# GpSimd adds lam ahead of the first logarithms of the large blocks, one logarithm for a quarter of the heads

## The chip, the core and the metric

The kernel runs on one core of one Trainium2 chip. The metric is the device time of one execution in microseconds. A core has five engines, each with its own queue of instructions, worked off in order: TensorE (PE in the profile), VectorE (DVE), ScalarE (ACT), GpSimd (POOL) and SyncE (SP, which issues the DMAs here).

## The reference, cut to what matters

Two layers follow each other on x of 8 images x 512 rows x 128 columns. The second, a six-layer local attention with feed-forward parts, is not touched. The first is an attention of 16 heads whose weights are not a softmax: each row's lam is found by four Newton steps, and the weight is 1/(lam - s).

```python
s = jnp.einsum('bhnd,bhmd->bhnm', Q, K) * scale
lam = s_masked.max(-1) + 1.0
for _ in range(num_iter):          # 4
    d = jnp.maximum(lam[..., None] - s, EPS)
    w = jnp.where(mask, d ** (-q), 0.0)          # q = 1
    f = w.sum(-1) - 1.0
    fp = -q * jnp.where(mask, d ** (-q - 1.0), 0.0).sum(-1)
    lam = lam - f / fp
d = jnp.maximum(lam[..., None] - s, EPS)
p = jnp.where(mask, d ** (-q), 0.0)
p = p / p.sum(-1, keepdims=True)
return jnp.einsum('bhnm,bhmd->bhnd', p, V)
```

## The kernel before

The first part, which ends about 1,620 us after the start, works on blocks. A block is 128 rows of one image, all 16 heads; block rb sees W = (rb + 1) x 128 keys, so blocks 3 and 2 are the large ones (W = 512 and 384) and blocks 1 and 0 the small ones. The heads of a block are worked on in four tiles, j = 0 to 3, of four heads each ("a quarter of the heads"). A partition holds a row and a head; in the free dimension lie four pieces a = 0 to 3, one per 32 rows, of 416, 448, 480 and 512 elements in block 3 (1,856 in all) and of 288, 320, 352 and 384 in block 2 (1,344), because later keys are left out. `ns` holds the negated scores, `lam` one number for each partition and piece.

A Newton step on one tile is Ln(ns + lam), then exp(-x), which gives 1/d, then sums by `bn_stats` (line 301); when the four tiles are done, a chain of small VectorE operations (lines 305 to 316) gives the new `lam`. How `lam` is added differs by size:

- Small blocks (`few`, line 290): GpSimd adds it, with `add_lam` (line 264), into tiles `df`, of which there are four; one Ln on ScalarE (line 294) then covers the whole tile.
- Large blocks: ScalarE adds it as the bias of the logarithm. The bias is one number per partition, so each of the four pieces needs a Ln of its own (line 298). The result goes to a tile `d` of the pool `dp`, which has two buffers (line 115). One Exp (line 299) then covers the whole tile.

After the last step the weights proper are made in the same way: `attend_add` (line 318) lets GpSimd add `lam` into a tile `da`, of which there are three; `attend_weigh` does Ln and Exp on ScalarE (lines 325, 326); `attend_sum` transposes on TensorE (line 339), masks on VectorE (line 342), multiplies with the values (line 351).

The loop goes over stages w (line 392). A stage is two blocks of one image: blocks 3 and 0, then blocks 2 and 1, then the next image. In stage w three things run side by side, in each of the steps k = 0 to 3: the Newton step k of the stage's two blocks, tile k of the weights and sums of the blocks of the stage before (`before`), and tile k of the scores of the blocks of the next stage (`nxt`, lines 238 to 257, written to `ns` by VectorE at line 254). The first `lam` of a stage (`first_lam`, lines 270 and 272) needs the smallest `ns` of all four tiles. `add_lams` (line 276) puts the small block's adds for one k ahead. At the change to the stage of blocks 2 and 1 the next image is projected (`project`, line 191): normalisation (`rstd` at line 97, `xn` at 102, copies `xnT` at 107), products with the weights (`qj` at 199, `kn` at 205), after which its scores can begin. When a block is done, `attend_end` copies `oT` on ScalarE (line 378) for the output product.

The order of the instructions on each engine is set by the scheduler that builds the program; it interleaves the parts of a step. Each engine then keeps to that order, and waits where an operand or a buffer is not ready. A tile's buffer is ready when all readers of its former content are done: for `d`, the `bn_stats` of two tiles earlier.

Of the kernel before, what the change touches and what calls it, by code (L numbers as in the profile page):

```python
# [49 lines left out]
def tile_kernel(  # L50
# [59 lines left out]
    with ExitStack() as c1:  # L110
# [111 lines left out]
        def keys(W, a):  # L222
            return W - Q * (3 - a)

        def pieces(d, W):

            at = [sum(keys(W, c) for c in range(a)) for a in range(5)]
            return [d[:, at[a] : at[a + 1]] for a in range(4)]
# [30 lines left out]
        def add_lam(t, d, j):  # L259

            W = t["W"]
            for a, (o, n) in enumerate(zip(pieces(d, W), pieces(t["ns"][j], W))):
                by = t["lam"][:, 4 * j + a : 4 * j + a + 1]
                nc.gpsimd.tensor_tensor(o, n, by.to_broadcast([P, keys(W, a)]), ALU.add)  # L264
# [19 lines left out]
        def newton(t, k):  # L284
            W, lam = t["W"], t["lam"]

            st = sm.tile([P, H, 2, 3], F32, name="stw")
            for j in range(4):
                ns = t["ns"][j]
                few = W <= 2 * P  # L290
                d = t["df"][j] if few else dp.tile([P, 4 * W - 6 * Q], F32, name="d")
                dv, nv = pieces(d, W), pieces(ns, W)
                if few:
                    nc.scalar.activation(d, d, AF.Ln)
                else:
                    for a in range(4):
                        c = 4 * j + a
                        nc.scalar.activation(dv[a], nv[a], AF.Ln, bias=lam[:, c : c + 1])  # L298
                nc.scalar.activation(d, d, AF.Exp, scale=-1.0)  # L299
                for a in range(4):  # L300
                    nc.vector.bn_stats(st[:, 4 * j + a].rearrange("p u k -> p (u k)"), dv[a])  # L301

            mean = st[:, :, :, 1]
            s1 = sm.tile([P, H, 2], F32, name="s1")
            nc.vector.tensor_tensor(s1, mean, st[:, :, :, 0], ALU.mult)
            q2 = st[:, :, :, 0]
            nc.vector.tensor_tensor(q2, s1, mean, ALU.mult)
            sw2 = sm.tile([P, H], F32, name="sw2")
            nc.vector.tensor_reduce(sw2, st[:, :, :, 0:3:2], axis=AX.XY, op=ALU.add)
            sw = sm.tile([P, H], F32, name="sw")  # L310
            nc.vector.scalar_tensor_tensor(
                sw, s1[:, :, 0], -1.0, s1[:, :, 1], ALU.add, ALU.add
            )
            nc.vector.reciprocal(sw2, sw2)
            nc.vector.tensor_tensor(sw, sw, sw2, ALU.mult)
            nc.vector.scalar_tensor_tensor(lam, sw, 0.0, lam, ALU.max, ALU.add)  # L316
# [75 lines left out]
        for w in range(len(work) + 1):  # L392
            before, now, nxt = now, nxt, []
            if w + 1 < len(work):
                b, rbs = work[w + 1]
                nxt = [block(b, rb, proj) for rb in rbs]
            for t in now:
                first_lam(t)
            for k in range(NUM_ITER):
                if now:  # L400
                    add_lams(now[1])
                for u in range(2):
                    if before:
                        attend_add(before[u], k)
                    if nxt:
                        scores(nxt[u], k)
                    if now:
                        newton(now[u], k)
                    if ready:
                        attend_sum(*ready)  # L410
                        ready = None
                    if before:
                        attend_weigh(before[u])
                        ready = (before[u], before[u]["d"], k)
            if w + 2 < len(work) and work[w + 2][1][0] == 3:
                if ready:
                    attend_sum(*ready)
                    ready = None
                proj = project(work[w + 2][0])
# [375 lines left out]
    t = -1  # L795
# [94 lines left out]
```

## Time and profile before

Three runs took 5203.93, 5205.71 and 5205.83 us, a median of 5205.71. The profiled execution took 5202.6 us, of which 5200.9 us are its span from the first to the last instruction.

| engine | busy us | share of the span | instructions |
|---|---|---|---|
| PE | 4371.9 | 84% | 44173 |
| DVE | 4428.0 | 85% | 11788 |
| ACT | 3822.1 | 73% | 6698 |
| POOL | 3204.4 | 62% | 3919 |

How to read the lines that follow. Times are microseconds from the start of the span unless marked ns. The rows of slices cut the span into 40 equal pieces, and each digit is the busy share of an engine in one of them, in tenths, 9 standing for 90% and more. A row of a table by window has the window, its length, then busy time with the number of instructions in brackets for PE, the weight loads of PE, DVE, ACT and POOL, then the granted TensorE clock, the DMA share and GB/s. A row of a group has the line, the engine, the operation, output and input with their sizes, the count, the busy time in us, the mean in ns and the idle time of the engine just before. A row of a timeline has the start, the length of what was merged, the engine, the line, the operation and the count; in square brackets stands the time that the engine was idle before it, and who ended it.

### The profile page before, as it was taken

Reading aid. Unit: us, or ns where it says so; the run is one execution under the profiler, and the core shown is the slowest. Engines: PE = TensorE matmul, PEld = TensorE weight load, DVE = VectorE, ACT = ScalarE, POOL = GpSimd, SP = SyncE. Lnnn points to the kernel's source line nnn. Section 1 sums busy time; section 2 is a strip of 40 time slices with the busy share of each in tenths; the row PEclk is TensorE's granted clock in tenths of the full one; section 3 lists DMA queues with packets and bytes.
Section 4 is the critical chain, followed back from the end, with each engine's and each line's share of the span. In section 5 each row is a group of like instructions: output and inputs, shape, how many; then the busy total and the mean of one; then the engine's idle time right before and its main releaser. Section 6 shows DMA issues by size and latency. Waiting matters only on the chain.

```text
span 5200.9 us, 116009 instructions
## 1 busy us (share of the span) xinstructions
PE 4371.9 (84%) x44173; PEld 2617.0 (50%) x44173; DVE 4428.0 (85%) x11788; ACT 3822.1 (73%) x6698; POOL 3204.4 (62%) x3919
## 2 busy tenths in 40 slices
PE   4556656556555999999999999999999999999998
PEld 1223322233323566666666666666666666666665
DVE  7788889888887888888888888888888888888886
ACT  6899989899997566666666666666666666666665
POOL 2444434435445777777777777677777777776774
PEclk7666667667666999999999999999999999999999
DMA  0000000000001211221212112121112212122121
GB/s 9 1 5 1 5 5 1 5 5 1 3 3 33 50 46 42 53 55 40 48 40 62 42 45 50 45 58 38 47 45 58 50 38 51 44 56 54 44 55 37
DMA packets 115041, 177.85 MB, mean 34 GB/s; under 512 B 13072, under 2 KB 38456, under 8 KB 114488
## 3 DMA queue, kind: packets, MB, share of 16 engines
q1 hardware_dynamic: 114488, 170.45, 13.4%
q8 instruction: 351, 5.75, 0.5%
q14 instruction: 202, 1.65, 0.1%
HBM read 21.52 MB, written 4.19 MB: 5 GB/s over the span
## 4 chain that ended last, share of the span: by engine, by line
DVE 37%; PE 33%; ACT 20%; POOL 6%; issue 3%; DMA 0%; ACTq 0%; POOLq 0%; SPq 0%; DVEq 0%
DVE qr L556 6%; DVE ss L546 6%; PE m L540 5%; DVE qn L548 5%; DVE stw L301 5%; ACT d L298 4%; DVE rs L640 3%; PE po L662 3%; PE pv L576 3%; ACT d L299 3%; PE pT L652 3%; PE acc L675 3%; PE s L623 2%; PE y L746 2%; PE s L249 2%
## 5 line engine op out<-in xcount | busy, mean ns | idle before, releaser
L560 POOL TENSOR_TENSOR qn<-qn,qr 128x512 f32<-128x512 f32 x768 | 975.3, 1270 | 447.6 <-DVE qr L556 316.0
L642 POOL TENSOR_TENSOR pr<-pr,rs 128x768 f32<-128x768 f32 x384 | 564.1, 1469 | 502.7 <-DVE rs L641 249.9
L568 POOL TENSOR_TENSOR qn<-qn,ss 128x512 f32<-128x512 f32 x768 | 784.6, 1042 | 56.6 <-ACT ss L565 56.4
L540 PE MATMUL m<-wqkv,xs 128*128 128x512 f32 x1536 | 751.5, 607 | 76.7 <-ACT qT L604 66.5
L264 POOL TENSOR_TENSOR df<-ns,lam 128x32 f32<-128x32 f32 (+7 forms) x1024 | 396.9, 425 | 607.9 <-DVE lam L316 388.0
L546 DVE TENSOR_REDUCE ss<-sq 128x8 f32<-128x512 f32 x768 | 521.2, 679 | 255.9 <-ACT sq L545 254.2
L298 ACT ACTIVATE d<-ns,lam 128x416 f32<-128x416 f32 (+7 forms) x1024 | 559.5, 615 | 65.9 <-DVE stw L301 28.4
L556 DVE TENSOR_TENSOR qr<-m,tab 128x256 f32<-128x256 f32 x1536 | 570.9, 412 | 0.0
L669 ACT COPY oT<-po 128x512 f32<-128x512 f32 x384 | 223.9, 583 | 460.9 <-PE po L662 460.9
L301 DVE BATCH_NORM_STATS2 stw<-d 128x6 f32<-128x416 f32 (+7 forms) x1024 | 514.6, 561 | 55.4 <-ACT d L299 54.9
L249 PE MATMUL s<-kn,qj 32*32 32x160 f32 (+15 forms) x4096 | 423.7, 492 | 152.0 <-DVE mn L254 137.5
L339 PE MATMUL dTp<-ident,da 128*128 128x128 f32 x1280 | 295.4, 372 | 294.0 <-issue 71.8
L548 DVE TENSOR_TENSOR qn<-m,tab 128x512 f32<-128x512 f32 x768 | 514.0, 669 | 0.0
L264 POOL TENSOR_TENSOR da<-ns,lam 128x416 f32<-128x416 f32 (+15 forms) x512 | 310.6, 638 | 329.1 <-PE dTp L339 253.9
L640 DVE TENSOR_REDUCE rs<-pr 128x8 f32<-128x768 f32 x384 | 363.6, 947 | 171.5 <-ACT pr L634 171.5
L545 ACT ACTIVATE sq<-m 128x512 f32<-128x512 f32 x768 | 433.7, 602 | 66.0 <-PE m L540 52.6
L604 ACT COPY qT<-ptq 128x512 f32<-128x512 f32 x768 | 414.0, 583 | 83.5 <-PE ptq L599 78.7
L599 PEld LDWEIGHTS ptq<-ident,qn 128*128 128x128 f32 x3072 | 359.1, 141 | 218.9 <-issue 113.6
L662 PE MATMUL po<-prT,v 96*64 96x64 f32 x12288 | 443.2, 225 | 0.1
L653 ACT COPY prT<-pT 96x512 f32<-96x512 f32 x768 | 428.0, 587 | 13.2 <-PE pT L652 7.8
L576 PE MATMUL pv<-wqkv,xs 128*128 128x512 f32 x768 | 432.8, 645 | 0.5 <-DVE qr L556 0.5
L634 ACT ACTIVATE pr<-pr 128x768 f32<-128x768 f32 x384 | 326.7, 851 | 136.4 <-DVE pr L630 135.5
(139 smaller groups left out, 9252.2 us busy)
## 6 DMA issues: line engine op xcount, KB each, us to landing
v<-v SPq DMA_DIRECT2D x192, 512.0 KB
v<-v SPq DMA_DIRECT2D x96, 256.0 KB
v<-v SPq DMA_DIRECT2D x96, 192.0 KB
wqkv<-in_L_ffn_Wqkv_dram SPq DMA_DIRECT2D x36, 256.0 KB
wo<-in_L_ffn_Wo_dram SPq DMA_DIRECT2D x12, 256.0 KB
xb<-in_L_attn_x_dram SPq DMA_DIRECT2D x8, 256.0 KB
x<-xb SPq DMA_DIRECT2D x8, 256.0 KB
xr<-x SPq DMA_DIRECT2D x8, 256.0 KB
```

Source lines behind the costliest of these rows:

```text
L264: nc.gpsimd.tensor_tensor(o, n, by.to_broadcast([P, keys(W, a)]), ALU.add)
L298: nc.scalar.activation(dv[a], nv[a], AF.Ln, bias=lam[:, c : c + 1])
L301: nc.vector.bn_stats(st[:, 4 * j + a].rearrange("p u k -> p (u k)"), dv[a])
L540: nc.tensor.matmul(m.rearrange("p h e -> p (h e)"), lhsT=lhsT, rhs=wqkv[:, t, :], start=True, stop=True,)
L546: nc.vector.tensor_reduce(ss[:, t, :], sq, axis=AX.X, op=ALU.add)
L548: nc.vector.tensor_tensor(qc, m, tab[:, 2 * t, c, :].unsqueeze(1).to_broadcast([P, HH, DHL]), ALU.mult)
L556: nc.vector.tensor_tensor(qr[:, :, u, :], mh[:, :, 1 - u, :], sw.unsqueeze(1).to_broadcast([P, HH, hd]), ALU.mult,)
L560: nc.gpsimd.tensor_tensor(qc, qc, qr.rearrange("p h u e -> p h (u e)"), ALU.add)
L568: nc.gpsimd.tensor_tensor(qc, qc, ss[:, t, :].unsqueeze(2).to_broadcast([P, HH, DHL]), ALU.mult)
L576: nc.tensor.matmul(pv, lhsT=lhsT, rhs=wqkv[:, 2, :], start=True, stop=True,)
L642: nc.gpsimd.tensor_tensor(flat, flat, rs.unsqueeze(2).to_broadcast([P, 2 * NT, KB]), ALU.mult)
L662: nc.tensor.matmul(po[e * DHL : (e + 1) * DHL, n * QB : (n + 1) * QB], lhsT=g["v3"][:, n, h * DHL : (h + 1) * DHL], rhs=prT[:, e, n // 2, ...
```

## The change

At the first Newton step (k = 0) of a large block GpSimd adds `lam` to the tile's four pieces, into the same `d`, by the helper that the small blocks use; ScalarE then does one Ln in place over the whole tile. The steps k = 1 to 3 and the small blocks are as before. No buffer count changes.

```diff
                 few = W <= 2 * P
                 d = t["df"][j] if few else dp.tile([P, 4 * W - 6 * Q], F32, name="d")
                 dv, nv = pieces(d, W), pieces(ns, W)
-                if few:
+                if k == 0 and not few:
+                    add_lam(t, d, j)
+                if few or k == 0:
                     nc.scalar.activation(d, d, AF.Ln)
                 else:
                     for a in range(4):
```

## The prediction

> **What bounds the kernel.** The page came first, for the part that the change touches. In the row of slices one slice is 130 us; the first 12 to 13 of 40 (0 to about 1,620 us) are the first part, with ScalarE (ACT) at 9 tenths, VectorE (DVE) at 8, GpSimd (POOL) at 4.
>
> ```profile
> DVE  7788889888887888888888888888888888888886
> ACT  6899989899997566666666666666666666666665
> POOL 2444434435445777777777777677777777776774
> ```
>
> A table of busy time by window then gave one period, two stages or one image. ACT is busy 184.9 of 201 us, POOL 89.4: GpSimd looks half free.
>
> ```profile
> 700.00:901.00 201.00, 119.28 (x1052) 60.44 (x1044) 172.34 (x632) 184.86 (x268) 89.37 (x194) 0.69 0.01 4
> ```
>
> Next the groups by form, for prices (last numbers: busy us, mean ns, idle before):
>
> ```profile
> L299 ACT ACTIVATE d<-d 128x1856 f32<-128x1856 f32 x128 | 222.3, 1736 | 0.0
> L298 ACT ACTIVATE d<-ns,lam 128x512 f32<-128x512 f32 x128 | 90.5, 707 | 0.0
> L264 POOL TENSOR_TENSOR da<-ns,lam 128x512 f32<-128x512 f32 x32 | 33.2, 1036 | 0.0
> ```
>
> The timelines were last, since an average cannot say where the 8% of ACT's idle time sits. It sits at the stage changes, and the longest piece there already waits for GpSimd:
>
> ```profile
> 733.27 1.53 ACT L298 ACTIVATE d<-ns,lam 128x320 f32<-128x320 f32 x3
> 738.95 1.75 ACT L325 ACTIVATE da<-da 128x1856 f32<-128x1856 f32 x1 [4.14 <-POOL da L264]
> ...
> 774.55 0.90 ACT L294 ACTIVATE df<-df 128x832 f32<-128x832 f32 x1 [2.71 <-POOL df L264]
> ```
>
> The same 4.14 stands at 537.98, 939.96 and 1141.16, one period apart. So ACT bounds the first part by its work, but at k = 0 of the stage of blocks 2 and 1 it is held by GpSimd, and that is the k which gets more GpSimd work.
>
> **What the change removes.** Four logarithms of a piece each become one over the whole tile, for 16 large blocks x 4 tiles: 192 ACT instructions less. From recorded means, block 3 has 631+654+680+707 = 2,672 ns against 1,736 (one activation of 1,856), block 2 has 524+548+575+602 = 2,249 against 1,311: 0.94 us each, 60 us for 64. But records overlap. Starts are what counts:
>
> ```profile
> 698.98 2.40 ACT L298 ACTIVATE d<-ns,lam 128x416 f32<-128x416 f32 x4
> 701.29 0.45 ACT L299 ACTIVATE df<-df 128x320 f32<-128x320 f32 x1
> 701.65 1.73 ACT L299 ACTIVATE d<-d 128x1856 f32<-128x1856 f32 x1
> 703.28 0.81 ACT L294 ACTIVATE df<-df 128x320 f32<-128x320 f32 x2
> ```
>
> Four take 701.29-698.98 = 2.31 us, one takes 703.28-701.65 = 1.63: 0.68. For block 2, 1.86 (797.98 to 799.84) against 1.22: 0.64. So 32 x 0.68 + 32 x 0.64 = **42 us** at most.
>
> **What it adds.** Four adds per tile on GpSimd: 876+929+982+1,036 = 3.82 us for block 3, 664+717+770+824 = 2.98 for block 2 by the means, 3.70 and 2.86 by a run of four on the timeline (780.36; 843.49). 32 x 3.70 + 32 x 2.86 = **210 us** on POOL, 13 us per stage, all in one quarter of it. No DMA or TensorE work is added or moved. The order of the changed program's instructions shows the adds and the 192 missing logarithms, so the change does what it says.
>
> The new wait: ACT's logarithm waits for POOL's adds, and POOL's adds for a `d` buffer. There are two, so tiles 0 and 1 can be filled once the statistics (L301) of tiles 2 and 3 of the last k have read theirs; tiles 2 and 3 must wait for the statistics of tiles 0 and 1. POOL is in order. Its new queue at k = 0 of blocks 2 and 1 is: d0, df0, d1, df1 to df3, da (block 3), da (block 0), three pieces of the next da, the memsets, d2, one piece of da, d3.
>
> **The stage of blocks 2 and 1, on the clock of before.** POOL now:
>
> ```profile
> 725.25 2.00 POOL L264 TENSOR_TENSOR df<-ns,lam 128x160 f32<-128x160 f32 x4 [9.53 <-DVE stw L301]
> 729.31 5.94 POOL L264 TENSOR_TENSOR df<-ns,lam 128x160 f32<-128x160 f32 x12 [2.06 <-DVE sw L309]
> 735.21 5.64 POOL L264 TENSOR_TENSOR da<-ns,lam 128x416 f32<-128x416 f32 x9
> ```
>
> - POOL: the buffer for d0 is free at 724.0 (statistics at 721.72, 2.27 us). d0 to 726.9, df0 728.9, d1 731.7, df1 to df3 737.7, da of block 3 741.3 (before 738.9), da of block 0 742.4, next da 745.2, memsets 746.6, d2 749.5, da 750.4, d3 753.3. No gap: 29 us of adds against some 15 of ACT's own work.
> - ACT: d0 and d1 are ready when it comes (729 to 733.5), but da is not until 741.3, d2 749.5, d3 753.3. In before the last log of tile 3 ended at 751.0; here it is 754.4. The 2.6 us saved are gone, and more.
> - Behind the log of d2 stand the two normalisations (`rstd`, L97). They ran at 742.6; now they come at 750.6. From there before's chain takes 748.7-742.6 = 6 us to the copy of `xnT`, 756.4 to `kn` and 760.8 to the first new `ns`. With +8 the `ns` come at about 768.5. In DVE's queue the block-1 update of `lam` stands behind them. Before has it at 772.2; now fewer statistics remain behind `ns` (about 3 us made up): 777.7. The 2.71 stall above is the wait for that update: the adds then end at 780.0 instead of 774.5, and ACT goes on to its next logs at 782.8 instead of 777.3, with 0.36 of work done ahead. **+5.1 us** for each of the 6 such stages with a projection. From there ACT has no idle time until 835 in before, so nothing gives it back.
> - In the two without it (first and last image) only the later da: 741.3-738.9 = **+2.4** each.
>
> **The stage of blocks 3 and 0.** d0 runs 826.5 to 830.2 and d1 to 833.9, hidden under the small block's activations. df0, da and df1 then end 2.1 us later than before; DVE's `ns` waits for that da (837.08 now, 1.11 idle) and goes to 839.1, the update of `lam` behind it to 842.0. POOL's next da needs that: 844.1; the one after it 847.0; d2 850.7; d3 854.4. ACT wants d2 at 847.2, waits 3.5 us, and also gets the copy `oT` 2 us later (841 for 839). Its k = 1 starts at 862.7 against 861.2: +1.5. I add 0.5 for the port below: **+2.0**, seven times.
>
> **The first stage.** Nothing hides it: `lam` is there at 42; the POOL queue has two pieces, 16 small adds (4.47), two pieces: d0 at 50.3, where before started its logs at 42.0. d1 54.0, d2 (after statistics) 63.2, d3 66.9, k = 1 at 74.5 against 63.1: **+11.4**.
>
> **A rule against the change.** The row: four DVE ops on `lam` beside busy POOL took 1.79 us at 822.05 (L272), two with POOL idle 0.36 at 694.39. The Trainium skill, "SBUF — State Buffer", section "Who interferes with whom", says that a VectorE instruction with two SBUF inputs and a GpSimd instruction that reads SBUF exclude each other, the later one waiting for the whole other. By the rule each of the 5 two-input ops of an update can wait up to one add (1.04 us): 5 us per update, 80 over the stages. By the row it is 0.45-0.18 = 0.27 each, 1.3 per update, half of it on the path: 0.5 in each stage of blocks 3 and 0, as taken. Statistics have one input and took 2.27 at 712.82 with POOL busy and 2.26 at 717.88 without.
>
> **Sum.** 11.4 + 2 x 2.4 + 7 x 2.0 + 6 x 5.1 = 60.8. On the profiled execution's 5,202.6 (span 5,200.9 and 1.7 around it) that is 5,263; the median shown is 3.1 above it, so 5,266. I take **5,265**. The second part has the same order of instructions and starts that much later.
>
> **Rivals.**
> 1. GpSimd is really half free. If d2 and d3 are ready when ACT gets there (in the stage of blocks 2 and 1 before about 745; the point is whether POOL leaves da by 739), ACT gets all 42 us: 5,164. For it: 89.4 busy of 201. Against: the 4.14 stall, and no gap in the queue from 724. 0.08.
> 2. The losses and the 42 us cancel: delays of k = 0 are taken up by waits of k = 1 (1.98 at 876.69 for DVE statistics). 5,195 to 5,216. 0.10.
> 3. The port as the rule has it: 80 us on top in place of my 3.5, 5,340; half of it 5,300. For it: the 1.79. Against: the projection's `xn` beside POOL took 2.28 for four instead of 1.12, doubled, not more. 0.10.
> 4. The forecast, 5,235 to 5,290 with its walks off by half: 0.72.
>
> A measurement of this kernel tells 0.2%, 10 us, from no change. Faster 0.10 (the first rival and an edge of the second), within 0.08, slower 0.82. The range leaves out the first rival and the far end of the third: 5,205 to 5,300.
>
> **What would show it.** In the profile of the changed kernel: ACT waiting for `POOL d L264` at k = 0, more on d2 and d3 than on d0; POOL without a gap for some 29 us at each change to blocks 2 and 1; the wait for da above 4.14; `rstd` some 8 us later after the stage's start; the small blocks' log at k = 1 waiting longer than 2.71; ACT's busy time in a period down by 7.5 recorded us, the period longer by 7. Wrong if the period is shorter than 201, or if ACT's new waits are for DVE.

## The result, and the profile after

Four runs of the changed kernel took 5282.70 to 5287.89 us, a median of 5286.40; four of the kernel before took 5197.57 to 5205.83, a median of 5204.82. The ratio is 1.0159, with a 95% interval of 1.0141 to 1.0176: the change costs 81 us. The profiled execution has a span of 5283.7 us.

The head of the changed kernel's page, busy time by engine and three of its rows of slices:

```profile
PE 4413.4 (84%) x44173; PEld 2611.8 (49%) x44173; DVE 4459.7 (84%) x11788; ACT 3784.3 (72%) x6506; POOL 3412.0 (65%) x4175
...
DVE  6788888888887888888888888888888888888886
ACT  5888888897888566666666666666666666666665
POOL 3645565456465677767777767777777777677674
```

ScalarE has 192 instructions and 37.8 us less, GpSimd 256 and 207.6 us more, as the diff says. VectorE has the same count and is busy for 31.7 us more. ScalarE's row, mostly 9s in the first part before, is now mostly 8s: it does less, and waits more. For what, the list of ScalarE's waits of the changed kernel up to 1,720 us says (total us, times, longest):

```profile
ACT d L296 <- POOL d L264: 68.7, 27, 4.7
ACT da L327 <- POOL da L264: 61.1, 8, 7.8
ACT df L296 <- POOL df L264: 44.9, 14, 13.3
ACT oT L380 <- PE pT L378: 36.0, 8, 5.2
```

Before (up to 1,640 us) da took 32.6, df 22.5, oT 13.7, and the first row did not exist. Three of the four rows end at GpSimd, 174.7 us against 55.1.

The time is lost a little in nearly every stage. I take a stage from the first logarithm of its large block to that of the next stage, and average six stages of each kind (the third to the eighth of blocks 3 and 0, the second to the seventh of blocks 2 and 1). Stages of blocks 3 and 0 went from 96.61 to 100.78 us, of blocks 2 and 1 from 104.01 to 110.76. That is 25.0 and 40.5 us for six of each; the first stage's end comes 13.1 later, the two stages between it and the averaged ones lose 1.4, and some 2 us are left for the rest.

The timelines of the changed kernel in one stage of blocks 2 and 1 show how, first ScalarE, then GpSimd (start, length, operation, count, in brackets the wait before it):

```profile
766.66 1.31 ACT L296 ACTIVATE d<-d 128x1344 f32<-128x1344 f32 x1
...
779.02 1.75 ACT L327 ACTIVATE da<-da 128x1856 f32<-128x1856 f32 x1 [7.84 <-POOL da L264]
...
787.00 1.32 ACT L296 ACTIVATE d<-d 128x1344 f32<-128x1344 f32 x1 [3.21 <-POOL d L264]
788.23 0.47 ACT L97 ACTIVATE rstd<-mv,eps_ln 128x4 f32<-128x4 f32 x2
790.80 1.32 ACT L296 ACTIVATE d<-d 128x1344 f32<-128x1344 f32 x1 [0.70 <-POOL d L264]
...
818.49 0.90 ACT L296 ACTIVATE df<-df 128x832 f32<-128x832 f32 x1 [4.33 <-POOL df L264]
```

```profile
761.82 2.86 POOL L264 TENSOR_TENSOR d<-ns,lam 128x288 f32<-128x288 f32 x4 [8.18 <-DVE stw L303]
764.63 2.00 POOL L264 TENSOR_TENSOR df<-ns,lam 128x160 f32<-128x160 f32 x4
766.59 2.85 POOL L264 TENSOR_TENSOR d<-ns,lam 128x288 f32<-128x288 f32 x4
769.40 5.92 POOL L264 TENSOR_TENSOR df<-ns,lam 128x160 f32<-128x160 f32 x12
775.28 7.49 POOL L264 TENSOR_TENSOR da<-ns,lam 128x416 f32<-128x416 f32 x11
782.70 0.22 POOL L207 MEMSET va<- 128x64 f32 x1
782.78 1.36 POOL L208 MEMSET va<- 128x1472 f32 x1
784.10 2.87 POOL L264 TENSOR_TENSOR d<-ns,lam 128x288 f32<-128x288 f32 x4
```

GpSimd has no gap from 761.82 to 790.8. The adds for tile 2 (784.10) begin when the instruction ahead of them ends, so it is the queue that makes them late and not the `d` buffer. ScalarE comes to da at 771.2 and to the logarithm of tile 2 (d2) at 783.8, and stands each time.

### The profile page after: what moved, and what is told of

It reads as the page before. It is cut to its first block, busy times and chain, and to the rows that moved or that the text cites. A ratio compares the mean times of both kernels' runs of the same rounds, so it can differ in the third digit from the quotient of the medians.

```text
span 5283.7 us, 116170 instructions
## 1 busy us (share of the span) xinstructions
PE 4413.4 (84%) x44173; PEld 2611.8 (49%) x44173; DVE 4459.7 (84%) x11788; ACT 3784.3 (72%) x6506; POOL 3412.0 (65%) x4175
## 4 chain that ended last, share of the span: by engine, by line
DVE 39%; PE 34%; ACT 15%; POOL 8%; issue 3%; DMA 0%; ACTq 0%; POOLq 0%; SPq 0%; DVEq 0%
DVE stw L303 6%; DVE qr L558 6%; DVE ss L548 5%; PE m L542 5%; DVE qn L550 5%; PE s L249 4%; DVE rs L642 3%; PE po L664 3%; PE pv L578 3%; ACT d L300 3%; PE pT L654 3%; PE acc L677 3%; PE s L625 2%; PE y L748 2%; ACT prT L655 2%
## 5 line engine op out<-in xcount | busy, mean ns | idle before, releaser
L249 PE MATMUL s<-kn,qj 32*32 32x384 f32 (+15 forms) x4096 | 453.2, 504 | 114.8 <-DVE mn L254 103.7
L300 ACT ACTIVATE d<-ns,lam 128x448 f32<-128x448 f32 (+7 forms) x768 | 419.3, 615 | 43.2 <-DVE lam L318 28.0
L655 ACT COPY prT<-pT 96x512 f32<-96x512 f32 x768 | 428.0, 587 | 12.6 <-PE pT L654 7.1
```

What stands on the lines that cost most here:

```text
L249: nc.tensor.matmul(s[a][rows, 0 : keys(W, a)], lhsT=qj[rows, j, q0 : q0 + Q], rhs=kn[rows, 0 : keys(W, a)], start=True, stop=True,)
```

## The experiments

The theory is the prediction's: the adds lengthen GpSimd's in-order queue where others wait for it, and ScalarE's saving is lost in waits. The rivals are that the merged logarithms do matter, that load counts wherever it lies, and, from run 9 on, that the granted TensorE clock (a share of full speed, as in the window rows) is the cause. The letters are explained where they stand.

Each ratio is to the kernel before on the same chip, with its 95% interval; times are medians, so the two can differ a little. Medians of before lay between 5203.42 and 5205.85 us. The diffs are to the changed kernel unless said.

### 1. The single logarithm without the adds

```diff
                 if k == 0 and not few:
-                    add_lam(t, d, j)
-                if few or k == 0:
+                    nc.scalar.activation(d, ns, AF.Ln, bias=high)   # high: a constant
+                elif few:
```

> At k = 0 of the large blocks one logarithm covers the whole tile, with one constant as its bias, and nobody adds lam there: lam is left out of that step's logarithm, so the step does not do Newton's arithmetic. GpSimd has no more work than before, ScalarE has all 192 instructions less. Theory Q (the loss is GpSimd's queue at the stage changes, the saving on ScalarE is real): faster than before, but not by the whole 42 us, since what is saved ahead of the 4.14 us wait for da in the stages of blocks 2 and 1 only lengthens that wait (2 x 0.64 us x 8): 5,165 to 5,180 us. Theory M (ScalarE's saving at k = 0 is worth nothing, because other engines end last there): within 10 us of before.

5209.77 us, ratio 1.0007 (1.0001 to 1.0014). M had the time. The stages show that it is made of two halves: the first stage need not wait for `lam`, starts 15.4 us earlier and ends 11.1 earlier, and then stages of blocks 3 and 0 take 99.34 us (before 96.61) and stages of blocks 2 and 1 105.55 (before 104.01). ScalarE has the 192 logarithms less, and it waits for others. From its timeline, two of the stalls:

```profile
679.91 2.93 ACT L302 ACTIVATE d<-ns,lam 128x416 f32<-128x416 f32 x5 [2.17 <-DVE lam L320]
...
737.24 1.75 ACT L329 ACTIVATE da<-da 128x1856 f32<-128x1856 f32 x1 [5.25 <-POOL da L266]
```

The first is for VectorE's `lam`, the second was 4.14 in the kernel before. So the saving on ScalarE came to nothing in the steady stages, even without the adds.

### 2. The adds, with the four logarithms kept

```diff
-                if few or k == 0:
+                if few:
```

> GpSimd adds lam into d as in the changed kernel, and ScalarE then overwrites d with the four logarithms of before, with lam as bias: the adds' cost without their gain. Theory Q: ScalarE waits for the adds of tiles 2 and 3 anyway, so only the logarithms of these two tiles show, 2 x 0.66 us x 16 stages = 21 us on top of the changed kernel: 5,300 to 5,315 us. If all of the 42 us were effective in the changed kernel: 5,328. Theory P (the loss is VectorE's small operations waiting for the shared port): no difference from Q here.

5288.33 us, ratio 1.0161 (1.0146 to 1.0176): 2 us above the changed kernel, not the 14 to 29 expected. With run 1 this says from both sides that the logarithms hardly matter, and that the 81 us are the price of the adds. The 2 us are a net figure: the instructions stand in another order than in the changed kernel, and the clock at the start of the stages of blocks 3 and 0 was 0.67 here and 0.50 there (table below), so the logarithms may be worth more than they show.

### 3. The same adds in another form of instruction

```diff
-                nc.gpsimd.tensor_tensor(o, n, by.to_broadcast([P, keys(W, a)]), ALU.add)
+                nc.gpsimd.tensor_scalar(o, n, by, None, ALU.add)   # the new adds only
```

> The new adds alone are done as tensor_scalar (one tensor input, lam as a scalar per partition) instead of tensor_tensor with lam broadcast. The order of the instructions on GpSimd is the same as in the changed kernel. If an add gets half as long (the Trainium skill has one-input operations on GpSimd at about line rate), theory Q: every stage's chain of adds gets some 5 to 6 us shorter, and nearly all of it is on the path: 5,190 to 5,215 us. Theory P: the adds still read SBUF and VectorE's updates still meet them, only the time of the wait halves: 5,240 to 5,260 us. If the add is not shorter, no change from the changed kernel by either.

5387.87 us, ratio 1.0353 (1.0337 to 1.0368). The premise, which is that of the Trainium skill ("GPSIMD Engine Reference", section "Engine selection"), did not hold here: with one tensor input the add is longer. Two groups of this run, the new adds and the old da adds (us in all, mean ns):

```profile
L265 POOL TENSOR_SCALAR d<-ns,lam 128x512 f32<-128x512 f32 x32 | 50.2, 1569 | 0.0
L267 POOL TENSOR_TENSOR da<-ns,lam 128x512 f32<-128x512 f32 x32 | 33.2, 1038 | 0.0
```

It turned into a test of dose. By the means the new adds take 5.78 us for a tile of block 3 in place of 3.82, and 4.54 in place of 2.98 for block 2: 32 x 1.96 + 32 x 1.56, about 112 us more on GpSimd. The order of the instructions was that of the changed kernel on every engine, and the kernel took 101 us more. An engine that is busy for 65% of the span passed nine tenths of this added work on to the end. It was added where the queue is already late; no run put the same work at another place of the queue, so that the place is the reason is argued, not shown.

The run also speaks against theory P. Its page:

```profile
PE 4431.7 (82%) x44173; PEld 2617.7 (49%) x44173; DVE 4437.1 (82%) x11788; ACT 3786.4 (70%) x6506; POOL 3527.5 (65%) x4175
```

VectorE is busy for 22.6 us less than in the changed kernel, only 9.1 more than before, and yet the time went up.

### 4 and 5. One large block alone

```diff
-                if k == 0 and not few:
+                one = k == 0 and W == 4 * P        # run 5: W == 3 * P
+                if one:
                     add_lam(t, d, j)
-                if few or k == 0:
+                if few or one:
```

> The change for block 3 alone; block 2 as before. From the stage lengths in the two traces: 13 us at the first stage and 3.7 to 5.1 in each later stage of blocks 3 and 0 belong to it, 38 to 40 us in all: 5,240 to 5,250 us if the stages' losses are separate (Q). If the late work of the stage of blocks 2 and 1 spills into the next stage, less than that: 5,220 to 5,235 us.

5214.99 us, ratio 1.0022 (1.0014 to 1.0030): below both.

> The new adds and the single logarithm for block 2 alone; block 3 as before. The queue theory (S: the stage of blocks 2 and 1 loses because GpSimd's queue is full at its start, and in the changed kernel it lost 6.75 us, some 2 of it handed over by the late stage ahead) expects 4 to 6 us for each of six stages, 2 in the two others and nothing in the first: 5230 to 5245. If the two blocks' losses simply add up (A), block 3 alone having cost 11 us of the 82, this costs 65 to 75: 5265 to 5280. If it is nothing by itself (N, only both together lose): within 10 us of before.

5252.88 us, ratio 1.0092 (1.0078 to 1.0107), between S and A. Together they cost 58 us, and the whole change 81. The lengths of stages, with the granted TensorE clock from 5 to 25 us after the start of a stage, mean of six. The last column is the sum of the two lengths, the time of one image. It is the firmer number: where an edit makes the scheduler order the instructions otherwise, work moves over the mark between the stages (before, the two kinds hold 470 and 570 of TensorE's instructions; in runs 1, 6 and 8 they hold 502 and 538).

| kernel | blocks 3 and 0, us | clock | blocks 2 and 1, us | clock | both, us |
|---|---|---|---|---|---|
| before | 96.61 | 0.80 | 104.01 | 0.59 | 200.6 |
| changed | 100.78 | 0.50 | 110.76 | 0.50 | 211.5 |
| 1: one logarithm, no adds | 99.34 | 0.62 | 105.55 | 0.62 | 204.9 |
| 2: adds, four logarithms | 101.66 | 0.67 | 110.45 | 0.50 | 212.1 |
| 3: longer adds | 107.87 | 0.59 | 117.36 | 0.50 | 225.2 |
| 4: block 3 alone | 98.50 | 0.51 | 102.78 | 0.63 | 201.3 |
| 5: block 2 alone | 97.46 | 0.78 | 110.78 | 0.51 | 208.2 |
| 6: block 2, tiles 0 and 1 | 97.15 | 0.69 | 106.99 | 0.51 | 204.1 |
| 7: block 2, tiles 2 and 3 | 97.32 | 0.74 | 108.78 | 0.50 | 206.1 |
| 8: before, da by bias | 98.19 | 0.62 | 106.14 | 0.51 | 204.3 |
| 9: before, TensorE kept busy | 110.41 | 0.85 | 103.52 | 0.87 | 213.9 |
| 10: changed, TensorE kept busy | 105.87 | 0.88 | 108.72 | 0.72 | 214.6 |
| 12: changed, kept busy at the start | 98.93 | 0.83 | 112.76 | 0.50 | 211.7 |

Block 2 alone makes the whole loss of its own stage, 6.77 of 6.75 us: S was wrong that 2 us of it are handed over by the stage before. Block 3 alone lengthens its own stage by 1.9 us, and the stage that follows is 1.2 shorter, all six at a clock of 0.63; the kernel before takes as long where its clock there is 0.64 (run 11 below). With block 2's adds nothing is given back.

### 6 and 7. Two tiles of block 2

```diff
+                one = k == 0 and W == 3 * P and j < 2       # in place of run 5's; run 7: j >= 2
```

> Of block 2 only tiles 0 and 1 get the new adds: they stand in GpSimd's queue ahead of the add for da of block 3, and nothing new stands in front of the logarithms of tiles 2 and 3 or of rstd. S expects only the later da (2.4 us): 8 stages x 1.5 to 2.4, 5215 to 5225, and da waited for some 6.5 us. If GpSimd's load is what counts, wherever it lies (L), half of what block 2 alone costs, the same as for tiles 2 and 3.

> Of block 2 only tiles 2 and 3 get the new adds: they stand behind both da adds in GpSimd's queue, so da comes as before (wait 4.14), but the logarithm of tile 2 comes some 5 us later, and rstd of the next image's projection behind it. S expects 3.5 to 5 us for each of six stages with a projection and little in the two others: 5225 to 5240, more than for tiles 0 and 1. L: the same as for tiles 0 and 1. If rstd has slack (N), within 5 us of before.

Run 6: 5252.38 us (six runs, 5224.65 to 5253.26; the profile is of the fastest), ratio 1.0075 (1.0057 to 1.0092). Run 7: 5241.99 us, ratio 1.0071 (1.0059 to 1.0083). ScalarE's waits at the start of a stage of blocks 2 and 1 are those that the two places in the queue ask for. Run 6:

```profile
754.22 1.75 ACT L328 ACTIVATE da<-da 128x1856 f32<-128x1856 f32 x1 [7.84 <-POOL da L264]
```

Run 7:

```profile
753.29 1.75 ACT L328 ACTIVATE da<-da 128x1856 f32<-128x1856 f32 x1 [4.14 <-POOL da L264]
...
761.26 1.32 ACT L297 ACTIVATE d<-d 128x1344 f32<-128x1344 f32 x1 [4.84 <-POOL d L264]
```

Adds ahead of da delay da alone; adds behind it leave da at 4.14 and delay tile 2. The stages of blocks 2 and 1 grew by 3.0 and 4.8 us (expected 1.5 to 2.4, and 3.5 to 5). By the whole times, though, run 6 lies far above its range and is not below run 7 (which is what L says of the two), and its six runs spread over 29 us, where the changed kernel's four spread over 5. That spread is what runs 9 to 12 are about.

### 8. The reverse, at one place of the kernel before

The diff is to the kernel before.

```diff
+            t["bias"] = j if j == 0 and t["W"] == 4 * P else None
+            if t["bias"] is None:
                 add_lam(t, d, j)
...
+                for a, (o, n) in enumerate(zip(pieces(d, W), pieces(t["ns"][j], W))):
+                    c = 4 * j + a
+                    nc.scalar.activation(o, n, AF.Ln, bias=t["lam"][:, c : c + 1])
```

> The reverse of the change at one place: the kernel before, but for the first weights tile of block 3 (da, k = 0) lam goes in as the bias of four logarithms on ScalarE, and GpSimd's four adds, for which ScalarE waited 4.14 us at each change to the stage of blocks 2 and 1, are gone. 0.68 us more of ScalarE work for each of 8 images. S expects 2 to 4 us less for each of seven stages: 5176 to 5192, with the wait for da gone and the next wait elsewhere. If another wait takes its place at once (W, as with the free adds of the merge-only run): 5200 to 5210.

5216.26 us, ratio 1.0022 (1.0015 to 1.0030). The stall of 4.14 us is gone, and the kernel is 10 us slower, above W's range too; the added logarithms, 0.68 us for each image, are some 5 of it. ScalarE's waits for statistics went from 28.4 to 54.9 us, for `lam` from 26.4 to 44.4. Taking a visible stall away gained nothing; both kinds of stages are longer than before, at a lower clock.

### 9 and 10. TensorE kept busy everywhere

Both kernels with this added after the statistics of each Newton tile (`bank` also holds `po`, which has the same shape as before):

```diff
+                nc.tensor.matmul(
+                    bank[0:24, P:], lhsT=st[:, 4 * j : 4 * j + 4].rearrange("p h u k -> p (h u k)"),
+                    rhs=far[:, 0 : 3 * P], start=True, stop=True,
+                )
```

> The kernel before with idle TensorE work added: after the statistics of each Newton tile one more product of 384 columns, read by nobody, 512 in all. It is to keep TensorE's granted clock from falling to 0.5 at the stage changes. The clock theory (C: part of the times is set by whether TensorE runs at half clock while the first tiles of a stage are transposed, as in the run with tiles 0 and 1 of block 2, where the one period of 201.4 us had 0.84 there and the others, of 204.8 us, had 0.64) expects a granted clock above 0.75 over the first part and 5170 to 5205. If the clock is a mere companion (Q), the added products only stand in TensorE's queue: 5205 to 5260.

> The changed kernel with the same added TensorE work. C: the clock no longer drops to 0.50 at the start of the stage of blocks 3 and 0, the half of that stage's 4.2 us goes, and the gap to the kernel before with the same work is 50 to 70 us in place of 81. Q: the gap stays at 75 to 90, or the waits for GpSimd's d and da are unchanged.

5291.32 us (ratio 1.0170, 1.0152 to 1.0188) and 5317.08 us (1.0218, 1.0200 to 1.0235). The mean granted clock of the whole profiled execution rose from 0.89 and 0.88 to 0.94 and 0.93, but the added products stand in TensorE's queue and cost 88 us in the kernel before, which is above both ranges. The gap between the two kernels fell from 81 to 26 us, below both theories. Of the 18 us between the two profiled executions 12.6 are there at the end of the first stage; afterwards an image takes 213.9 and 214.6 us, almost the same. So the price of the adds is no property of GpSimd's queue alone: it depends on which other waits end last. As the added products bring waits of their own (ScalarE's for `lam` rose from 26.4 to 74.9 us in the kernel before) and another order of the instructions, the runs don't separate C from Q.

### 11. Run 6's kernel again, for a second profile

> The kernel with the adds on tiles 0 and 1 of block 2 once more, for a second profile: its six runs took from 5224.65 to 5253.26 us. C: if this one is near 5252, its instruction order is the same, its periods are longer by 3 to 5 us each, and the granted clock early in the stage of blocks 3 and 0 is 0.5 to 0.6 in every period. Against C: the longer periods have the same clock there as the period of 201.4 us, 0.84.

5235.06 us. From the second on, the stages of blocks 3 and 0 of the two profiles, fourteen in all, have one order of instructions on ScalarE, GpSimd and TensorE, and in each 138 products fall in the window from 5 to 25 us. Three such windows of run 6 (busy us and counts of PE, weight loads, DVE, ACT, POOL, then the granted clock):

```profile
648.73:668.73 20.00, 18.58 (x138) 8.67 (x137) 14.35 (x45) 18.27 (x28) 6.87 (x13) 0.62 0.01 1
853.54:873.54 20.00, 14.41 (x138) 7.01 (x137) 17.13 (x61) 18.22 (x28) 6.95 (x13) 0.84 0.00 1
1464.47:1484.47 20.00, 16.05 (x138) 7.66 (x137) 15.59 (x48) 19.65 (x29) 6.88 (x13) 0.79 0.01 1
```

These stages took 98.13, 94.74 and 95.85 us. TensorE does the same 138 products in 18.58 or in 14.41 us. In the second profile the stage at 0.84 took 94.77, that at 0.79 took 96.27, and of the four at 0.61 and 0.62 the three in mid-course 98.00 to 98.22. The time of the stage goes with the clock, with the same instructions in the same order. The run came between the two ends of the six earlier ones, and its clock is low in most of its stages, not in every one: C had the direction, and was too simple.

The kernel before shows it too. Three windows at the same place of its stages of blocks 2 and 1:

```profile
733.98:753.98 20.00, 9.49 (x46) 6.43 (x42) 13.55 (x35) 15.23 (x25) 12.23 (x21) 0.57 0.09 26
934.99:954.99 20.00, 9.68 (x46) 6.48 (x42) 13.36 (x35) 15.21 (x25) 12.23 (x21) 0.56 0.09 26
1136.19:1156.19 20.00, 8.69 (x47) 5.83 (x44) 14.36 (x37) 15.25 (x25) 12.24 (x21) 0.64 0.09 27
```

They took 104.77, 104.95 and 102.61 us. In the changed kernel all twelve stages of the table start at 0.50. One group of products at the start of a stage of blocks 3 and 0 there, at a clock of 0.50, and its like in the kernel before, at 1.00 (the last numbers are busy us, mean ns and idle us):

```profile
L249 PE MATMUL s<-kn,qj 32*32 32x352 f32 x8 | 2.4, 789 | 0.0
```

```profile
L249 PE MATMUL s<-kn,qj 32*32 32x352 f32 x8 | 1.3, 457 | 0.0
```

The window of the table ends at 25 us, and hides something in the stages of blocks 2 and 1. From 20 to 40 us after their start the clock was 0.76 to 0.91 before, and 0.50 to 0.51 in the changed kernel. That it goes with time there too, run 7 shows. Two such windows, of stages with one order of instructions on all four engines:

```profile
557.20:577.20 20.00, 13.96 (x109) 8.40 (x113) 17.58 (x52) 17.90 (x25) 2.85 (x7) 0.78 0.05 15
763.33:783.33 20.00, 14.90 (x68) 8.65 (x72) 15.52 (x40) 15.73 (x20) 2.85 (x7) 0.56 0.05 14
```

These stages took 107.83 and 110.00 us. So the clock may have a part in what the changed kernel loses in both kinds of stages. The late adds also leave TensorE less to do there (42 products in that window against 118 to 150 before), so the low clock may itself be one of their results. No run tells these apart.

### 12. TensorE kept busy only at the start of the stage of blocks 3 and 0

```diff
+        def busy(lam):
+            for _ in range(2):
+                nc.tensor.matmul(bank[0:H, P:], lhsT=lam, rhs=far[:, 0 : 3 * P], start=True, stop=True)
...
+            if k == 3 and W in (2 * P, 3 * P):    # end of newton
+                busy(lam)
...
+            if t["W"] in (P, 4 * P):              # end of first_lam
+                busy(lam)
```

> The changed kernel with a little idle TensorE work only where a stage of blocks 3 and 0 begins: two products of 384 columns, read by nobody, behind each of four updates of lam there, 64 in all, so that TensorE has less of a gap before the stage's first transposes. C (the clock is a cause): the granted clock in the first 20 us of that stage, 0.50 in the changed kernel against 0.79 to 0.84 before, rises above 0.7, and the kernel gains 2 to 4 us in each of six periods: 5262 to 5276. Q (the clock is a companion; the loss is GpSimd's queue alone): the clock rises, and the time is 5282 to 5300. If the clock stays at 0.5, the run decides nothing.

5286.78 us, ratio 1.0156 (1.0139 to 1.0173): no gain, and Q had the time. The clock did rise, to 0.83, and the stages of blocks 3 and 0 became 1.9 us shorter (98.93); the stages of blocks 2 and 1 became 2.0 longer (112.76). Up to 1,720 us ScalarE waits 87.0 and 61.1 us for the GpSimd tiles d and da, 68.7 and 61.1 in the changed kernel. So a higher clock at that place doesn't bring the 81 us back. It is no clean test, though. In the averaged stages all of the added products run behind the mark, from 0.3 to 17.6 us after the first logarithm, and the instructions stand in another order than in the changed kernel on every engine. Whether the 1.9 us were a gain that something else ate, or only a shifted mark between the two stages, the run doesn't tell.

No version here beats the kernel before.

## Why the prediction was right, and where it was not

**Direction and main mechanism: right.** The adds cost through GpSimd's in-order queue at the start of a stage; how much of the size is the clock's is open. Measured from the first logarithm of the stage of blocks 2 and 1, the walk has da at 12.3 us, d2 at 20.5, d3 at 24.3 and `rstd` at 21.6; the timeline above has 12.36, 20.34, 24.14 and 21.57. GpSimd's 29 us without a gap came as written. Runs 2, 3 and 5 show the adds as a cause: the adds alone, the whole loss; more work at the same places of that queue, more time; block 2's adds alone, the loss of their stage. Runs 6 and 7 show the two places in the queue with their two stalls. What no run shows is that the same adds would cost less elsewhere in the queue.

**The step that failed: "So ACT bounds the first part by its work", and with it "42 us at most" as what the merge is worth.** Rival 1 was priced with it at 5,164. The merge is worth about 2 us under the adds (run 2), and without the adds the steady stages got longer, not shorter (run 1). At the stage changes ScalarE's free time goes into waits for da, `lam` and statistics. ScalarE's busy time fell by 37.8 us over the whole kernel, close to the 42 by starts; the sign "down by 7.5 recorded us" in a period (60 in all) was taken from the means, and busy time counts overlapping records once. The forecast itself did not lean on it, because its walks gave the saving away at each wait. Why the merge alone lengthens a stage by 1.5 to 2.7 us is open; the clock can be part of it in the stages of blocks 3 and 0 (0.62 for 0.80), and hardly in those of blocks 2 and 1, where it was 0.62 for 0.59.

**The size: 60.8 us summed, 81 measured.** The two profiled spans lie 82.8 apart. By terms:

- First stage, 11.4: measured 13.1. d0 was ready 9.0 us late, walked as 8.3; the rest of the stage lost 4.1, walked as 3.1.
- Stages of blocks 2 and 1, "+5.1 us" each: measured 6.75. The stage that I walked, from 728.98 us, took 104.77 before and 111.07 after, 6.3. The small block's log at k = 1 waits 4.33 (written: longer than 2.71) and comes at 51.83 instead of 45.57, 6.3 late where I had 5.5. Most of the other 0.4 lies in the reference: two of the six stages before had run at a clock of 0.64 and taken 102.6. The walk kept TensorE's durations of before, so the clock of 0.50 up to 40 us after the start is a candidate for what it missed.
- The two without a projection, "+2.4" each: the first lost 0.8 (109.59 for 108.79), the last and all that follows 2.7 together.
- Stages of blocks 3 and 0, "+2.0" seven times: the first of the seven lost 0.6, the other six 4.2 each, 25.6 in place of 14.0, the largest miss. The walk's chain was there: d2 waits 4.68, walked 3.5, and the copy `oT` comes 8.46 us after the start, before 5.26, walked 2 later. Changed, then before:

```profile
666.56 3.38 ACT L296 ACTIVATE d<-d 128x1856 f32<-128x1856 f32 x2
675.02 0.27 ACT L380 COPY oT<-pT 128x128 f32<-128x128 f32 x1 [5.08 <-PE pT L378]
...
686.05 1.75 ACT L296 ACTIVATE d<-d 128x1856 f32<-128x1856 f32 x1 [4.68 <-POOL d L264]
```

```profile
833.75 2.92 ACT L298 ACTIVATE d<-ns,lam 128x416 f32<-128x416 f32 x5
839.01 0.27 ACT L378 COPY oT<-pT 128x128 f32<-128x128 f32 x1 [2.35 <-PE pT L376]
```

  Here too the walk kept TensorE's durations of before, and in the changed kernel TensorE runs there at 0.50, not 0.80. The stage that lost 0.6 had 0.68 in the window, but also another order of instructions. With block 3 alone the stage grew by 1.9, close to the walk, though its clock was 0.51 in that window too; so the clock is a candidate for the rest, and not shown to be it.

**The port.** I took 0.5 us for seven stages, and the rule of the Trainium skill ("SBUF — State Buffer", "Who interferes with whom") as a rival of 40 to 80 us. Some single operations in the changed kernel's VectorE timeline do as the rule says (the first beside GpSimd's adds, the second without):

```profile
665.18 0.94 DVE L313 SCALAR_TENSOR_TENSOR sw<-s 128x16 f32<-128x16 f32 x1
...
698.51 0.17 DVE L313 SCALAR_TENSOR_TENSOR sw<-s 128x16 f32<-128x16 f32 x1
```

The difference, 0.77, is most of one add of 0.88 to 1.04 us, and more than the 0.27 of my row. Over all, VectorE is busy for 31.7 us more with 207.6 us of adds, and only a part of that can lie on the path. Rival 3 in full did not come, and in run 3 VectorE's excess fell to 9.1 us while the time rose by 101, so the port can hardly be the main cost. What part of the 20 us missed is the port's is not separated from the clock.

**Rival 2** (the losses cancel) is what run 4 shows for block 3 from its second stage on, not for block 2.

## What to carry to other kernels

Before work is given to an engine that is half idle, look at its queue at the place where the work goes: GpSimd was busy for 89 of 201 us, and yet 81 of the 208 us added came out at the end, and nine tenths of what run 3 put on top. All of it stood where others already waited; what the same work costs elsewhere in the queue was not tried. That its row shows 9 doesn't make an engine the bound: leave its work out in one run, and see whether the time moves. And where the granted clock moves, compare stages at equal clock and with one order of instructions before a few us per stage are put down to the edit.

## What the runs showed of the hardware

- GpSimd's add of one number per partition is slower as `tensor_scalar` (1,569 ns for 128x512 in run 3) than as `tensor_tensor` with a broadcast second input (1,038 ns in the same run).
- TensorE's granted clock differs between like stages of one execution, and their time goes with it: in run 6 94.74 us at 0.84 and 98.13 at 0.62, with the same 138 products in the window, though over the whole stage TensorE is busy for 54.95 and 59.44 us and ScalarE for 91. The Trainium skill, "TensorE: Matmul & The Clock Gate", section "Part 1: The HAM clock gate", has the clock follow TensorE's own activity, seen through a window that runs freely and does not start with the kernel. Like stages with unlike clocks fit that; the window itself no run here shows.
